# Attention terms of two graph layers: from row tiles on VectorE in the second, in four column groups of TensorE in the first

## The chip, the core and the metric

The kernel runs on one core of a Trainium2 chip. The core has TensorE (matrix products, into the accumulator memory PSUM), VectorE, ScalarE and GpSimd for elementwise work, and SyncE, which issues transfers. Each engine takes its own instructions in order and waits for the others by semaphores. In the profile they are PE (PEld is TensorE's loading of the stationary operand), DVE, ACT, POOL and SP. The metric is the time of one execution on the device in microseconds (us).

## What is computed

A graph network of two attention layers, followed by a transformer block (attention and a mixture of 8 experts), on 1250 nodes of 768 features, all in float32. The change is in the graph layers. Each does this, with 41,250 edges given as `src` and `dst`:

```python
def _gat_layer(x, W, a_src, a_dst, b, src, dst, n_nodes):
    h = x @ W
    e_src = h @ a_src
    e_dst = h @ a_dst
    e = jax.nn.leaky_relu(e_src[src] + e_dst[dst], NEG_SLOPE)
    m = jax.ops.segment_max(e, dst, num_segments=n_nodes)
    w = jnp.exp(e - m[dst])
    z = jax.ops.segment_sum(w, dst, num_segments=n_nodes)
    alpha = w / z[dst]
    out = jax.ops.segment_sum(h[src] * alpha[:, None], dst, num_segments=n_nodes)
    return out + b

h = _gat_layer(x, W1, att_src1, att_dst1, b1, src, dst, n_nodes)
h = jax.nn.relu(h)
out = _gat_layer(h, W2, att_src2, att_dst2, b2, src, dst, n_nodes)
```

The two attention terms of a node are `e_src` and `e_dst`. Since `h @ a = x @ (W @ a)`, the kernel never takes them from `h`: it computes the two vectors `W @ a_src` and `W @ a_dst` and multiplies the layer's input by them.

## The kernel before

Nodes are cut into NT = 10 tiles of T = 125, features into DC = 6 pieces of P = 128. Of a layer's input two forms occur: row tiles (125 nodes on partitions, 768 features along the row) and the transposed form `xT` (feature pieces on partitions, all 1250 nodes along the row). `CHUNKS` cuts the 1250 nodes into three pieces of 417, 417 and 416 columns.

**The vectors.** `attention_vectors` (L167) loads `a_src` and `a_dst` repeated on all partitions (`rep`) and has VectorE multiply every piece of `W` by them and sum (L183), twelve instructions a layer. The result, `wa`, has the features on partitions, two columns a piece.

**The terms.** `attention_terms` (L187) multiplies `xT` by these two columns, six matmuls a chunk that add up in PSUM (`pe`, L192), and ScalarE copies the two rows that come out into `er` (L195), which has 2 partitions and 1250 columns. It is a generator: each `next` issues one matmul. In the first layer two chunks are issued together (L361) ahead of the edge work (`win`, L364 to L380, and the transposes of `win`, L388), and the third is dealt out one matmul at a time among the counting of edges (L409 to L420: VectorE makes one-hot rows `ohp`, TensorE counts with 25 small matmuls `pc`). In the second layer all three chunks are issued together (L552) after the last tile of the first layer has been turned into `x1T`.

**A layer** (`gat_layer`, L472). Ten transposes turn `er` into `es`, nodes on partitions (`pec`, L479; copy L480). VectorE takes the largest source term per destination (`most`, L487 and L489, ten steps), from which come, by further turns and copies, the rows `rows` (L464 to L470). Then `rest()` projects the input, `h = x @ W` (`project`, `ph`, L203): seven tiles in the first layer, all ten in the second. Destination tiles are taken in three parts (4, 3 and 3 tiles). For each part ScalarE and VectorE make ten weight tiles `wt` (L517 to L522, 12 buffers), and for each destination tile TensorE adds up 20 matmuls (`pagg`, L529); VectorE divides (`rz`, L533) and adds the bias (`o`, L535). In the first layer `o` is transposed (`ptr`, L140) and ScalarE copies it through a ReLU into `x1T` (L297). With the first tile the second layer's weight `gw2` is loaded, over the first's, and its vectors are made (L549).

**What sets the order.** Tiles are written in program order, and a scheduler at build time fixes each engine's sequence by readiness and by that order. In the blocks under `manual_schedule` the order of the named engines is that of the code. The chip then runs each engine's sequence as it stands. A tile of a pool waits for its buffer: `gp` has two of each tag (`xr`, `row` for `o`, `e`), `gpt` has three PSUM buffers `tr` in the layers and two in the edge stage. Matmuls in float32 appear in the profile as two records each, transposes as one.

Of the kernel before, what the change touches and what calls it, by code (L numbers as in the profile page):

```python
# [10 lines left out]
F32 = mybir.dt.float32  # L11
# [6 lines left out]
ALU = mybir.AluOpType  # L18
AX = mybir.AxisListType
# [8 lines left out]
def gnn_ffn_kernel(  # L28
# [24 lines left out]
    nc = tc.nc  # L53
    N, D = x.shape
    E = src.shape[0]
    P = 128
    T = 125
    NT = N // T
    DC = D // P
# [42 lines left out]
    ident = const.tile([P, P], F32, name="ident")  # L102
# [57 lines left out]
    with tc.tile_pool(name="cnt", bufs=1) as cpool:  # L160

        cnt = cpool.tile([T, NT, N], U16, name="cnt")

        wa = cpool.tile([P, 2, DC, 2], F32, name="wa")
        er = cpool.tile([2, N], F32, name="er")

        def attention_vectors(layer, w, a_src, a_dst, pool, bufs):  # L167

            def load(a):
                rep = pool.tile([P, D], F32, tag="rep", name="rep", bufs=bufs)  # L170
                tc.keep_in_program_order((nc.sync if bufs > 1 else nc.scalar).dma_start(
                    rep, bass.AP(tensor=a.tensor, offset=a.offset, ap=[[0, P], [1, D]])))
                return rep

            reps = [load(a) for a in (a_src, a_dst)[:bufs]]
            if bufs > 1:
                yield None
            for i in range(2):
                if i == bufs:
                    reps.append(load(a_dst))  # L180
                for c in range(DC):
                    scr = pool.tile([P, D], F32, tag="scr", name="scr", bufs=1)
                    nc.vector.scalar_tensor_tensor(scr, w[:, c, :], 1.0, reps[i], op0=ALU.mult, op1=ALU.mult,  # L183
                                                   accum_out=wa[:, layer, c, i:i + 1])
                    yield None

        def attention_terms(layer, xT, psum):  # L187

            for c0, w in CHUNKS:
                pe = psum.tile([P, 4, P], F32, tag="tr", name="pe").rearrange("p a b -> p (a b)")  # L190
                for c in range(DC):
                    nc.tensor.matmul(pe[0:2, :w], wa[:, layer, c, :], xT[:, c, c0:c0 + w],  # L192
                                     start=(c == 0), stop=(c == DC - 1))
                    if c == DC - 1:
                        nc.scalar.copy(er[:, c0:c0 + w], pe[0:2, :w])  # L195
                    yield None

        def project(xT, w, h, psum, tiles):
# [16 lines left out]
        with tc.tile_pool(name="edge", bufs=1) as ep, \  # L215
# [53 lines left out]
            def find_rows():  # L269
                nc.vector.tensor_scalar(begun, nodes, head, None, ALU.is_gt)  # L270
                pk = epc.tile([P, 512], F32, tag="pc", name="pk")
                for t in range(NT):
                    nc.tensor.matmul(pk[:T, t:t + 1], begun[:, t * T:(t + 1) * T], oneb,
                                     start=True, stop=True)
                return pk

            def gather_row(t):
                krows[t] = op.tile([T, EC], F32, tag="kr", name="kr", bufs=LEAD)
                nc.gpsimd.indirect_dma_start(
                    out=krows[t], out_offset=None, in_=keys[0:E].rearrange("(p e) -> p e", p=T),  # L280
                    in_offset=bass.IndirectOffsetOnAxis(ap=row[:, t:t + 1], axis=0))
# [20 lines left out]
            xT = big.tile([P, DC, N], F32, tag="A", name="xnT")  # L302
# [4 lines left out]
            def spread(t):  # L307
                if t == len(xrows):
                    xn = op.tile([T, D], F32, tag="xn", name="xn", bufs=4)
                    split_rows(nc.sync if t % 2 == 0 else nc.scalar, xn, x[t * T:(t + 1) * T, :])  # L310
                    xrows.append(xn)
                stats[t] = ln_root(xrows[t])
# [14 lines left out]
            def vector(n):  # L327
                for _ in range(n):
                    next(vectors, None)

            fixed = {mybir.EngineType.PE, mybir.EngineType.DVE, mybir.EngineType.Pool}
            with tc.manual_schedule(engines=fixed):
                vector(1)
                pk = find_rows()
                spread(0)
                nc.vector.tensor_scalar(row, pk[:T, :NT], -1.0, None, ALU.add)
                nc.vector.tensor_scalar(edges, pk[:T, :NT], -1.0, float(EC), ALU.add, ALU.mult)
                for t in range(LEAD):
                    gather_row(t)
                nc.gpsimd.iota(upto, pattern=[[1, 2 * NT], [0, 5 * PG]], base=1, channel_multiplier=0,  # L340
                               allow_small_or_imprecise_dtypes=True)
                for t in range(4):
                    if t > 0:
                        spread(t)
                        normal(t - 1)
                normal(3)
                for t in range(4):
                    columns(t)
                for t in range(NT):
                    if 2 <= t <= 7:  # L350
                        spread(t + 2)
                    first_edges(t)
                    if t + LEAD < NT:
                        gather_row(t + LEAD)
                    if t % 3 == 0 and t // 3 < EARLY:
                        project(xT, gw, h, gpo, [t // 3])
                    vector(0 if t < 3 else 1 if t < 5 else 2)
                    if 2 <= t <= 7:
                        normal(t + 2)
                        columns(t + 2)  # L360
                terms = attention_terms(0, xT, gpt)  # L361
                for _ in range(2 * DC):
                    next(terms)
                nc.vector.tensor_tensor(win, win, node[:, :, None].to_broadcast([T, NT, SL]), ALU.subtract)  # L364
# [6 lines left out]
                                           accum_out=found)  # L371
# [12 lines left out]
            for u0 in range(0, NT // 2, 4):  # L384
                n = min(4, NT // 2 - u0)
                pt = gpt.tile([P, 4, P], F32, tag="tr", name="pl")
# [14 lines left out]
            with tc.manual_schedule(engines={mybir.EngineType.PE, mybir.EngineType.DVE}):  # L401
                for g in range(NP // PG):
# [12 lines left out]
                    for i in range(2):  # L415
                        c0 = (2 * u + i) * T + q0
# [34 lines left out]
        with tc.tile_pool(name="gwork", bufs=2) as gp, \  # L451
# [6 lines left out]
            def columns_to_rows(cols, o):  # L458

                for t0 in range(0, NT, 4):  # L460
# [8 lines left out]
                    else:  # L469
                        nc.scalar.copy(out_, pt[:T, :n, :T])  # L470

            def gat_layer(layer, rest, b):  # L472
                bias = gv.tile([T, D], F32, tag="bias", name=f"bias{layer}")
                nc.scalar.dma_start(bias, bass.AP(tensor=b.tensor, offset=b.offset, ap=[[0, T], [1, D]]))

                es = gv.tile([T, NT, 2], F32, tag="es", name=f"es{layer}")
                pt = gpt.tile([P, 4, P], F32, tag="tr", name="pec").rearrange("p a b -> p (a b)")
                for t in range(NT):
                    nc.tensor.transpose(pt[:T, 2 * t:2 * t + 2], er[:, t * T:(t + 1) * T], ident[0:2, 0:2])  # L479
                nc.scalar.copy(es.rearrange("p t i -> p (t i)"), pt[:T, :2 * NT])  # L480

                most = gv.tile([T, N], F32, tag="most", name=f"most{layer}")
                for t in range(NT):
# [4 lines left out]
                    else:  # L488
                        nc.vector.scalar_tensor_tensor(most, am[:, t, :], es[:, t, 0:1], most,  # L489
                                                       op0=ALU.add, op1=ALU.max)  # L490

                mx = gv.tile([T, NT], F32, tag="mx", name="mx")
                for t0 in range(0, NT, 4):
                    n = min(4, NT - t0)
                    pt = gpt.tile([P, 4, P], F32, tag="tr", name="pmx")
# [16 lines left out]
                for d0, nd in PARTS:  # L512
                    cs = slice(d0 * T, (d0 + nd) * T)
                    ws = []
                    for j in range(NT):
# [4 lines left out]
                                                       op0=ALU.min, op1=ALU.max)  # L520
                        wt = gp.tile([T, PW], F32, tag="wt", name="wt", bufs=12)
                        nc.vector.scalar_tensor_tensor(wt[:, :nd * T], e[:, 0, :nd * T], 1.0, cnt[:, j, cs],  # L522
                                                       op0=ALU.min, op1=ALU.mult)
                        ws.append(wt)
                    for d in range(d0, d0 + nd):
                        po = gpo.tile([T, 2, 512], F32, tag="po", name="pagg")
                        for s in range(2):
                            for j in range(NT):
                                nc.tensor.matmul(po[:, s, :DH + s], ws[j][:, (d - d0) * T:(d - d0 + 1) * T],  # L529
                                                 h[:, j, s * DH:(s + 1) * DH + s],  # L530
                                                 start=(j == 0), stop=(j == NT - 1))
                        rz = small.tile([T, 1], F32, tag="rz", name="rz")
                        nc.vector.reciprocal(rz, po[:, 1, DH:DH + 1])  # L533
                        o = gp.tile([T, D], F32, tag="row", name="o")
# [6 lines left out]
                project(xT, gw, h, gpo, range(EARLY, NT))  # L541
                return h

            x1T = None
            for t, o in gat_layer(1, rest_of_first, gb1):
                if t == 0:
                    x1T = big.tile([P, DC, N], F32, tag="A", name="x1T")
                    gw2 = load_big_weight(gW2, "gw2")
                    for _ in attention_vectors(1, gw2, ga_src2, ga_dst2, gp, 1):  # L549
                        pass  # L550
                transpose_rows(gpt, o, evict_to(x1T, t, AF.Relu))
            for _ in attention_terms(1, x1T, gpt):  # L552
                pass

            def all_of_second():
                h = node_rows("h2")
# [8 lines left out]
            pt = gpt.tile([P, 4, P], F32, tag="tr", name="pln")  # L565
# [3 lines left out]
            for t, o in gat_layer(2, all_of_second, gb2):  # L569
# [4 lines left out]
                xr = gp.tile([T, D], F32, tag="xr", name="xres")  # L574
# [208 lines left out]
    start = gate.tile([P, NE], F32, name="start")  # L783
# [27 lines left out]
    before = gate.tile([T, T], F32, name="before")  # L811
# [23 lines left out]
    with tc.tile_pool(name="proj", bufs=3, reuse_waits="tile") as pp, \  # L835
# [5 lines left out]
        w = load_expert(first_w, *expert(0))  # L841
# [81 lines left out]
        for t in range(NT):  # L923
            if t + 1 < NT:
# [8 lines left out]
                                       op0=ALU.add, op1=ALU.is_gt, accum_out=count)  # L933
# [10 lines left out]
    with tc.tile_pool(name="moe", bufs=2, reuse_waits="tile") as mp, \  # L944
# [66 lines left out]
        xr = fetch(xd[0:CAP, :], NS)  # L1011
# [21 lines left out]
        xT = turn(xr, NS)  # L1033
        for i, (e, n, _, _) in enumerate(jobs):
# [6 lines left out]
            if i + 1 < len(jobs):  # L1041
                _, m, ws, slots = jobs[i + 1]
                w = load_expert(mp.tile([P, 2 * DC * FF], F32, tag="w", name="we"), *ws)
                xr = fetch(slots(), m)
                xT = turn(xr, m)
# [33 lines left out]
```

## Time and profile before

| | us |
|---|---|
| median of 3 runs (lowest, highest) | 1541.48 (1539.98, 1541.97) |
| the profiled execution, on the device | 1540.1 |
| its span, first to last instruction | 1538.3 |

| engine | busy us | share of the span | instructions |
|---|---|---|---|
| PE | 1457.0 | 95% | 5981 |
| PEld | 782.8 | 51% | 5981 |
| DVE | 796.7 | 52% | 1285 |
| ACT | 597.8 | 39% | 950 |
| POOL | 433.9 | 28% | 287 |

Line groups that the change touches, in the profile's order: L192 `pe` in the first layer, 36 records, from 61.5 to 133.6 us; L192 in the second, 36 records, from 339.4 to 351.6; L479 `pec`, 10 records in each layer; L183 `scr`, 24 products of 0.957 us in both layers together, the second layer's from 208.6 to 224.0.

The graph layers take the first 581 us of the span. Shares are averages over stages with different limits: what an instruction costs is seen only where it stands in the chain of waits, that is, in the sequence of work followed back from the last instruction to whatever released each step. The granted TensorE clock over the whole span is 0.962 of full speed; it is at half in some stretches in which TensorE has little to do, the counting of edges among them.

### The profile page before, as it was taken

Reading aid. Unit: us, or ns where it says so; the run is one execution under the profiler, and the core shown is the slowest. Engines: PE = TensorE matmul, PEld = TensorE weight load, DVE = VectorE, ACT = ScalarE, POOL = GpSimd, SP = SyncE. Lnnn points to the kernel's source line nnn. Section 1 sums busy time; section 2 is a strip of 40 time slices with the busy share of each in tenths; the row PEclk is TensorE's granted clock in tenths of the full one; section 3 lists DMA queues with packets and bytes.
Section 4 is the critical chain, followed back from the end, with each engine's and each line's share of the span. In section 5 each row is a group of like instructions: output and inputs, shape, how many; then the busy total and the mean of one; then the engine's idle time right before and its main releaser. Section 6 shows DMA issues by size and latency. Waiting matters only on the chain.

```text
span 1538.3 us, 15938 instructions
## 1 busy us (share of the span) xinstructions
PE 1457.0 (95%) x5981; PEld 782.8 (51%) x5981; DVE 796.7 (52%) x1285; ACT 597.8 (39%) x950; POOL 433.9 (28%) x287
## 2 busy tenths in 40 slices
PE   5689999999999999999999999999988997799998
PEld 3376655555555555553444434334333665466565
DVE  4598633205326740117877877877888665011111
ACT  3222503202414621215655655655666354212121
POOL 6300000000000002004764664664666322122222
PEclk9856999999999999999999999999999997899999
DMA  7100010000021118940000000000030333745644
GB/s 215 32 1 31 11 72 0 0 11 2 1 81 56 56 44 338 408 175 23 1 21 1 21 0 21 1 21 1 0 101 1 126 118 120 292 166 179 222 150 142
DMA packets 48847, 125.49 MB, mean 82 GB/s; under 512 B 6103, under 2 KB 22680, under 8 KB 48768
## 3 DMA queue, kind: packets, MB, share of 16 engines
q1 hardware_dynamic: 30958, 55.99, 10.8%
q0 software_dynamic: 12688, 57.10, 9.8%
q10 hardware_dynamic: 5122, 11.36, 2.5%
q8 instruction: 48, 0.79, 0.2%
q14 instruction: 31, 0.25, 0.1%
HBM read 71.30 MB, written 57.60 MB: 84 GB/s over the span
## 4 chain that ended last, share of the span: by engine, by line
PE 70%; DVE 11%; issue 8%; DMA 5%; ACT 4%; POOL 1%; SPq 0%; POOLq 0%; DVEq 0%; ACTq 0%
PE pagg L529 12%; PE ph L203 8%; PE st L663 8%; PE pav L707 7%; PE pk L626 5%; PE pv L642 5%; PE phe L993 5%; PE poe L1002 5%; PE pq L626 4%; DVE sT L693 2%; DMA xd<-yn,slot 2%; PE pe L192 2%; PE pc L413 2%; PE po L851 2%; DMA xn<-in_x_dram 1%
## 5 line engine op out<-in xcount | busy, mean ns | idle before, releaser
L699 POOL TENSOR_TENSOR acc<-acc,sT 125x834 f32<-125x834 f32 (+1 forms) x139 | 273.2, 1965 | 10.9
L529 PE MATMUL pagg<-h,wt 125*125 125x385 f32 (+1 forms) x800 | 262.7, 486 | 0.4 <-DVE wt L522 0.4
L672 DVE TENSOR_TENSOR most<-most,st 125x834 f32<-125x834 f32 (+1 forms) x144 | 147.0, 1021 | 105.3 <-ACT sT L666 102.1
L529 PEld LDWEIGHTS pagg<-h,wt 125*125 125x125 f32 x800 | 147.4, 187 | 106.1 <-DVE wt L522 3.5
L693 DVE TENSOR_TENSOR sT<-sT,mb 125x834 f32<-125x834 f32 (+1 forms) x180 | 174.2, 1016 | 22.6 <-PE mb L688 22.6
L694 ACT ACTIVATE sT<-sT 125x834 f32<-125x834 f32 (+1 forms) x180 | 158.4, 900 | 49.0 <-DVE sT L693 48.6
L666 ACT COPY sT<-st 125x834 f32<-125x834 f32 (+1 forms) x180 | 151.7, 848 | 51.7 <-PE st L663 49.7
L663 PE MATMUL st<-qk 64*125 64x417 f32 (+1 forms) x720 | 163.7, 554 | 4.4 <-DVE most L672 4.3
L707 PE MATMUL pav<-sT,v 125*64 125x417 f32 (+1 forms) x720 | 151.5, 534 | 8.7 <-ACT sT L694 8.7
L604 POOL MEMSET zero<- 128x772 f32 x1 | 0.7, 742 | 520.6 <-PE ptr L140 520.6
L699 POOL TENSOR_TENSOR acc<-sT 125x834 f32<-125x834 f32 (+1 forms) x18 | 35.4, 1965 | 275.2 <-ACT sT L694 275.2
L663 PEld LDWEIGHTS st<-qk 64*125 64x125 f32 x720 | 56.3, 183 | 99.8 <-DVE most L672 43.4
L707 PEld LDWEIGHTS pav<-sT,v 125*64 125x64 f32 x720 | 42.7, 137 | 104.9 <-issue 43.7
L1002 PE MATMUL poe<-we,hT 128*128 128x384 f32 x264 | 88.8, 486 | 0.0
L626 PE MATMUL pq<-yT,wqk 128*128 128x417 f32 (+1 forms) x216 | 88.1, 534 | 0.0
L851 PE MATMUL po<-wp,aT 128*125 128x384 f32 x240 | 87.5, 498 | 0.0
L993 PE MATMUL phe<-xT,we 128*128 128x384 f32 (+1 forms) x288 | 86.6, 460 | 0.0
L1006 DVE SCALAR_TENSOR_TENSOR sofar<-poe,weight,sofar 128x768 f32<-128x768 f32 x25 | 25.4, 1018 | 116.8 <-PE poe L1002 109.8
L626 PE MATMUL pk<-yT,wqk 128*128 128x417 f32 (+1 forms) x216 | 84.0, 526 | 0.0
L203 PE MATMUL ph<-gw,xnT 128*125 128x384 f32 x240 | 82.5, 504 | 0.0
L642 PE MATMUL pv<-wv,yT 128*125 128x384 f32 x240 | 79.9, 490 | 1.4 <-issue 1.4
L203 PE MATMUL ph<-gw,x1T 128*125 128x384 f32 x240 | 78.6, 487 | 0.0
(219 smaller groups left out, 1737.1 us busy)
## 6 DMA issues: line engine op xcount, KB each, us to landing
xd<-zero POOLq DMA_DIRECT2D x8, 3860.0 KB
we<-in_L_ffn_W_dram SPq DMA_DIRECT2D x16, 1152.0 KB
xr<-xd SPq DMA_DIRECT2D x25, 386.0 KB
gw<-in_L_gnn_W_dram SPq DMA_DIRECT2D x2, 2304.0 KB
wqk<-in_L_ffn_Wqkv_dram SPq DMA_DIRECT2D x12, 384.0 KB
xres<-in_x_dram SPq DMA_DIRECT2D x10, 375.0 KB
xsd<-xres ACTq DMA_DIRECT2D x10, 375.0 KB
wv<-in_L_ffn_Wqkv_dram SPq DMA_DIRECT2D x1, 2304.0 KB
```

What stands on the lines that cost most here:

```text
L203: nc.tensor.matmul(po[:, s, :DH], xT[:, c, t * T:(t + 1) * T], w[:, c, s * DH:(s + 1) * DH], start=(c == 0), stop=(c == DC - 1))
L529: nc.tensor.matmul(po[:, s, :DH + s], ws[j][:, (d - d0) * T:(d - d0 + 1) * T], h[:, j, s * DH:(s + 1) * DH + s], start=(j == 0), stop=(j = ...
L626: nc.tensor.matmul(pq[:, :w], wqk[:, c, i, :], yT[:, c, c0:c0 + w], start=(c == 0), stop=(c == DC - 1))
L642: nc.tensor.matmul(pv[:T, s, :DH], yT[:, c, t * T:(t + 1) * T], wv[:, c, s * DH:(s + 1) * DH], start=(c == 0), stop=(c == DC - 1))
L663: nc.tensor.matmul(st[:T, i, :w], self.qk[r, 1, j * T:(j + 1) * T], self.qk[r, 0, self.c0:self.c0 + w], start=True, stop=True)
L666: nc.scalar.copy(s[:, :, :w], st[:T, :, :w])
L693: nc.vector.tensor_tensor(s[:, :, :w], s[:, :, :w], self.mb[:T, :, :w], ALU.subtract)
L694: nc.scalar.activation(s[:, :, :w], s[:, :, :w], AF.Exp)
L699: nc.gpsimd.tensor_tensor(self.acc[:, :, :w], prev[:, :, :w], s[:, :, :w], ALU.add)
L707: nc.tensor.matmul(self.pav[r, :w], v[:, j, hd0:hd0 + HD], s[:, i, :w], start=(j == 0), stop=(j == NT - 1))
L993: nc.tensor.matmul(ph[:, :n * P], w1[:, c, f * P:(f + 1) * P], xT[:, c, :n * P], start=(c == 0), stop=(c == DC - 1))
L1002: nc.tensor.matmul(po[:, d, :DH], hT[:, f, s * P:(s + 1) * P], w2[:, f, d * DH:(d + 1) * DH], start=(f == 0), stop=(f == FC - 1))
```

## The change

In the first layer the vectors lie in `wa1` with 32 columns a piece, of which 30 are zero, set once by GpSimd. The matmul of piece c now writes 32 PSUM partitions, beginning at 32 * (c % 4): four groups of partitions hold partial sums (pieces 0 and 4, 1 and 5, 2, 3). `er` has 128 partitions. The four partial sums are added when `er` is turned: in place of a transpose, a matmul with `four`, a 128 x 2 matrix of ones at the places of the two terms in each group, made from the identity.

In the second layer `attention_terms` and the turns of `er` are gone. The vectors `wa2` are turned after the first tile into rows repeated on 125 partitions, `wrow`: twelve transposes of a broadcast column (`pwr`), three copies by ScalarE. VectorE then takes both terms of a tile from its row tile `o`: ReLU, product and sum in one instruction for each term (`second_terms`), into `es2`, one tile behind the transposes. Its scratch, and the loads and scratch of `attention_vectors` in this layer, use the buffers of tag `xr`.

```diff
--- before.py
+++ after.py
@@ -161,13 +161,18 @@
 
         cnt = cpool.tile([T, NT, N], U16, name="cnt")
 
-        wa = cpool.tile([P, 2, DC, 2], F32, name="wa")
-        er = cpool.tile([2, N], F32, name="er")
-
-        def attention_vectors(layer, w, a_src, a_dst, pool, bufs):
+
+        wa1 = cpool.tile([P, DC, 32], F32, name="wa1")
+        nc.gpsimd.memset(wa1, 0.0)
+        wa2 = cpool.tile([P, 2, DC], F32, name="wa2")
+        er = cpool.tile([P, N], F32, name="er")
+
+        es2 = cpool.tile([T, NT, 2], F32, name="es2")
+
+        def attention_vectors(layer, w, a_src, a_dst, pool, bufs, tags=("rep", "scr")):
 
             def load(a):
-                rep = pool.tile([P, D], F32, tag="rep", name="rep", bufs=bufs)
+                rep = pool.tile([P, D], F32, tag=tags[0], name="rep", bufs=bufs if layer == 0 else None)
                 tc.keep_in_program_order((nc.sync if bufs > 1 else nc.scalar).dma_start(
                     rep, bass.AP(tensor=a.tensor, offset=a.offset, ap=[[0, P], [1, D]])))
                 return rep
@@ -179,20 +184,21 @@
                 if i == bufs:
                     reps.append(load(a_dst))
                 for c in range(DC):
-                    scr = pool.tile([P, D], F32, tag="scr", name="scr", bufs=1)
+                    scr = pool.tile([P, D], F32, tag=tags[1], name="scr", bufs=1 if layer == 0 else None)
                     nc.vector.scalar_tensor_tensor(scr, w[:, c, :], 1.0, reps[i], op0=ALU.mult, op1=ALU.mult,
-                                                   accum_out=wa[:, layer, c, i:i + 1])
+                                                   accum_out=wa1[:, c, i:i + 1] if layer == 0 else wa2[:, i, c:c + 1])
                     yield None
 
-        def attention_terms(layer, xT, psum):
+        def attention_terms(xT, psum):
 
             for c0, w in CHUNKS:
                 pe = psum.tile([P, 4, P], F32, tag="tr", name="pe").rearrange("p a b -> p (a b)")
                 for c in range(DC):
-                    nc.tensor.matmul(pe[0:2, :w], wa[:, layer, c, :], xT[:, c, c0:c0 + w],
-                                     start=(c == 0), stop=(c == DC - 1))
+                    g = c % 4
+                    nc.tensor.matmul(pe[32 * g:32 * g + 32, :w], wa1[:, c, :], xT[:, c, c0:c0 + w],
+                                     start=(c < 4), stop=(c + 4 >= DC))
                     if c == DC - 1:
-                        nc.scalar.copy(er[:, c0:c0 + w], pe[0:2, :w])
+                        nc.scalar.copy(er[:, c0:c0 + w], pe[:, :w])
                     yield None
 
         def project(xT, w, h, psum, tiles):
@@ -358,7 +364,7 @@
                     if 2 <= t <= 7:
                         normal(t + 2)
                         columns(t + 2)
-                terms = attention_terms(0, xT, gpt)
+                terms = attention_terms(xT, gpt)
                 for _ in range(2 * DC):
                     next(terms)
                 nc.vector.tensor_tensor(win, win, node[:, :, None].to_broadcast([T, NT, SL]), ALU.subtract)
@@ -469,15 +475,22 @@
                     else:
                         nc.scalar.copy(out_, pt[:T, :n, :T])
 
+
+            four = gv.tile([P, 2], F32, name="four")
+            nc.vector.tensor_reduce(four, ident.rearrange("p (g k) -> p k g", g=4)[:, 0:2, :], AX.X, ALU.add)
+
             def gat_layer(layer, rest, b):
                 bias = gv.tile([T, D], F32, tag="bias", name=f"bias{layer}")
                 nc.scalar.dma_start(bias, bass.AP(tensor=b.tensor, offset=b.offset, ap=[[0, T], [1, D]]))
-
-                es = gv.tile([T, NT, 2], F32, tag="es", name=f"es{layer}")
-                pt = gpt.tile([P, 4, P], F32, tag="tr", name="pec").rearrange("p a b -> p (a b)")
-                for t in range(NT):
-                    nc.tensor.transpose(pt[:T, 2 * t:2 * t + 2], er[:, t * T:(t + 1) * T], ident[0:2, 0:2])
-                nc.scalar.copy(es.rearrange("p t i -> p (t i)"), pt[:T, :2 * NT])
+                es = es2
+                if layer == 1:
+
+                    es = gv.tile([T, NT, 2], F32, name="es1")
+                    pt = gpt.tile([P, 4, P], F32, tag="tr", name="pec").rearrange("p a b -> p (a b)")
+                    for t in range(NT):
+                        nc.tensor.matmul(pt[:T, 2 * t:2 * t + 2], er[:, t * T:(t + 1) * T], four,
+                                         start=True, stop=True)
+                    nc.scalar.copy(es.rearrange("p t i -> p (t i)"), pt[:T, :2 * NT])
 
                 most = gv.tile([T, N], F32, tag="most", name=f"most{layer}")
                 for t in range(NT):
@@ -541,16 +554,34 @@
                 project(xT, gw, h, gpo, range(EARLY, NT))
                 return h
 
-            x1T = None
+            def second_terms(t, o):
+
+                for i in range(2):
+                    scr = gp.tile([T, D], F32, tag="xr", name="scr")
+                    nc.vector.scalar_tensor_tensor(scr, o, 0.0, wrow[:, i * D:(i + 1) * D], op0=ALU.max, op1=ALU.mult,
+                                                   accum_out=es2[:, t, i:i + 1])
+
+            x1T = before = None
             for t, o in gat_layer(1, rest_of_first, gb1):
                 if t == 0:
                     x1T = big.tile([P, DC, N], F32, tag="A", name="x1T")
                     gw2 = load_big_weight(gW2, "gw2")
-                    for _ in attention_vectors(1, gw2, ga_src2, ga_dst2, gp, 1):
+                    for _ in attention_vectors(1, gw2, ga_src2, ga_dst2, gp, 1, ("xr", "xr")):
                         pass
                 transpose_rows(gpt, o, evict_to(x1T, t, AF.Relu))
-            for _ in attention_terms(1, x1T, gpt):
-                pass
+                if t == 0:
+
+                    wrow = gv.tile([T, 2 * D], F32, name="wrow")
+                    flat = wa2.rearrange("p i c -> p (i c)")
+                    for k0 in range(0, 2 * DC, 4):
+                        pt = gpt.tile([P, 4, P], F32, tag="tr", name="pwr")
+                        for k in range(4):
+                            nc.tensor.transpose(pt[:T, k, :], flat[:, k0 + k:k0 + k + 1].to_broadcast([P, T]), ident)
+                        nc.scalar.copy(wrow[:, k0 * P:(k0 + 4) * P], pt[:T].rearrange("p a b -> p (a b)"))
+                else:
+                    second_terms(*before)
+                before = t, o
+            second_terms(*before)
 
             def all_of_second():
                 h = node_rows("h2")
```

## The prediction

> **What bounds it now.** I read the page's chain of waits first, then that chain for the first 470 us in order of time, then busy time by stage. The page's chain by engine:
>
> ```profile
> PE 70%; DVE 11%; issue 8%; DMA 5%; ACT 4%; POOL 1%; SPq 0%; POOLq 0%; DVEq 0%; ACTq 0%
> ```
>
> and the pieces of the chain around the change (start us, length us, engine, tile, line, records):
>
> ```profile
> 61.54 10.26 PE pe L192 x24
> 71.80 0.33 PE psum L376 x2
> ...
> 105.02 1.47 PE pe L192 x2
> ...
> 138.43 2.25 PE pec L479 x10
> 140.69 21.27 PE ph L203 x60
> ...
> 338.79 0.64 PE ptr L140 x6
> 339.43 12.69 PE pe L192 x36
> 352.11 4.71 PE ph L203 x14
> 356.82 0.17 PE pln L566
> 356.99 1.09 PE pec L479 x10
> ...
> 379.45 53.54 PE ph L203 x166
> 432.99 21.31 PE pagg L529 x66
> ```
>
> The reader is to see that both attention terms (L192) and both turns of `er` (L479) lie on the chain themselves, and that after the second terms TensorE goes on with `ph` until 433, with `pagg` right behind it. Busy time by stage (length, then PE, PEld, DVE, ACT, POOL with counts, granted clock, DMA share, GB/s) says the same:
>
> ```profile
> 72.40:136.50 64.10, 54.42 (x642) 44.51 (x642) 55.86 (x36) 16.95 (x52) 0.00 (x0) 0.53 0.01 2
> 136.50:200.00 63.50, 61.56 (x208) 37.87 (x209) 39.72 (x66) 25.15 (x42) 0.00 (x0) 0.94 0.07 25
> 200.00:339.00 139.00, 137.87 (x466) 81.34 (x465) 40.77 (x79) 25.72 (x51) 0.00 (x0) 1.00 0.06 20
> 339.00:433.00 94.00, 93.79 (x316) 51.57 (x315) 34.31 (x46) 28.05 (x48) 0.00 (x0) 1.00 0.02 5
> ```
>
> From 200 to 433 TensorE is full at clock 1.00 and VectorE is idle two thirds of the time. Work taken off TensorE here is time; work put on VectorE is not, as long as TensorE doesn't wait for it.
>
> **Second layer's terms leave TensorE: -13.8.** The 36 records of `pe` (12.69) and the 10 of `pec` (1.09) go: 13.78 us. What is late next? `es2` is whole two VectorE products after the last `o` (337.09 + 1.02): a product of this kind is L183, 0.957 and an accumulator read, 1.00 from start to start, so at 340.2, against 358.3 now. Today `wt` of all ten tiles of the first part is done at 396.0, 37.6 after `es`; then 378. `ph` would end at 433.0 - 13.8 = 419.2: 41 us of cover. Nothing becomes late; the shift goes through whole, because `pagg` waits for the end of `ph` both times.
>
> **The 20 products of `second_terms`: 0.** Two per tile, 2.0 us. VectorE waits 12.34 us for `pagg` in front of most `rz`, so they fit. At a change of part (248 to 262) VectorE refills `wt`; there the product for tile 3 may fall among them, but `wt` 8 and 9 are made at 256.2 and 257.3 and `pagg`, at 0.65 a tile from about 254.7, reaches them near 261. Were the cover gone, a tile would cost its 2.0. Each `o` now lives until the next tile's turn; two buffers do for that. Their scratch takes the two `xr` buffers, so the loads of `xres` that SP issued at 137.2 go out near 340; they are needed after 455.
>
> **Twelve turns `pwr`: +1.3.** Six `ptr` took 0.64, so 12 take 1.28, on a full TensorE. Three ScalarE copies of 128x512 (L470's of 125x500 are under 0.6) lie in ScalarE's idle. A wait is added: TensorE waits for `wa2`, and `pagg` of tile 1 stands behind it. VectorE now finishes the second half of those vectors at 223.96. If all 12 stand right behind `ptr` of tile 0 (which ends at 217.15), TensorE stands 6.8 us. Ends: +1.3 and +8.1. I take the lower: `ptr` of later tiles is put four records into the next tile's `pagg` and waits at most 0.57, tile 0's is put ten records in and waits for nothing, so the order given to TensorE follows VectorE's times well here.
>
> **First two chunks in column groups: -5.6.** Now 24 records one after another. With four groups, c = 0..3 run together and c = 4, 5 together: 2 rounds x 2 passes x 2 chunks = 8 slots. The weight loads show the record spacing: 0.35 for two, then 0.69 to 65.03 and 0.65 to 65.68 (the clock was at half there), then 0.35. Eight slots end at 66.03; `psum` starts at about 66.2, not at 71.80: 5.6 us. Behind it stands VectorE's `win` (L374), done at 65.66, so no more than 6.1 can come of it; `found` is there at 64.3.
>
> Is it so, side by side? No row has four groups. The nearest has two:
>
> ```profile
> 698.99 0.20 PEld L707 LDWEIGHTS pav<-sT,v 125*64 125x64 f32 x4 [0.60 <-ACT sT L694]
> 698.99 1.62 PE L707 MATMUL pav<-sT,v 125*64 125x417 f32 x8
> ```
>
> Eight records of the same 417 columns, 64 output partitions each, in 1.62: less the last one's 0.51, 1.11 us from the first start to the last, three spacings of 0.37 and not seven of 0.35 (2.45). So pairs start together, fp32 and all. [...] But all four loads above fall in 0.20 us while the first pair (0.51) runs: the row decides, 5.6. If only two groups ever run together, it is 12 slots: 67.4, a gain of 4.2. Ends: -2.9 (pairs and loads, with a margin) and -6.1.
>
> **Third chunk: +0.8.** Its six matmuls go one at a time into the count (`next(terms)` at g % 4 == 3), so nothing runs beside them; four are in the chain at 1.47. [...] The row between `st` (64 rows) and `pq` (128) shows 0.1 a change: 0.8, which I take. Ends 0 and 1.6.
>
> **`es1` by matmul: +1.1.** A transpose is one record, an fp32 matmul two (psum L376 is x2). Ten turns at half clock took 2.25; twenty records, each with a load of 125 columns, take about 4.4: +2.2. The clock hands some back: 60 `ph` in 21.27, against 0.3225 each later (96 in 30.96), means about six at 0.64. If the clock rises as long after the count as now, `pec` uses 2.2 us of that slow time, and 3.4 `ph` run at full clock instead: -1.1. Net +1.1; ends 0 and +3.4 (no refund, and TensorE waiting 1.2 for `four`, if that stands behind the ten L448 adds, done at 139.4). VectorE's `most` moves with it; `wt` has 12 us of cover before `ph` ends at 200.4.
>
> **At nothing:** the memset of `wa1` (POOL is idle from 7.8 to 14.5), the copies of `er` on 128 partitions in place of 2, `attention_vectors` on `xr` buffers (the second row still loads when the first six products are done).
>
> **Sum:** -13.8 - 5.6 + 1.3 + 0.8 + 1.1 = -16.2. The profiled execution took 1540.1 (span 1538.3 and 1.8 around it), so 1523.9; it stood 1.4 below the median of 1541.5, so against the median **1525.3**.
>
> **Rivals.**
> *The groups don't run side by side.* For it: no four-group row, fp32 in two passes. Against: `pav`. The 5.6 stays: 1530.9. Chance 0.13.
> *`pwr` holds TensorE up* by the 6.8 above, one early place in a queue that can't be passed: 1532.1. Chance 0.13.
> *Slower: VectorE's new filler stands ahead of `o`.* `second_terms` and the second layer's `most` (nine of its ten steps need only finished tiles, 1.53 each) may be put between `rz` and `o`. `ptr` is only four records (1.3 us) behind, so each us is TensorE's: 3.5 a tile over nine tiles, 31.8, gives 1557.1. It decides from 1.8 a tile. For it: the filler has no other engine. Against: in the trace `o` follows `rz` directly, even amid the `wt` refill. Chance 0.04.
> My forecast 0.68; 0.02 for what I don't see.
>
> **Range and chances.** Best ends: -13.8 - 6.1 + 1.3 + 0 + 0, and up to 1.9 of slow clock gone: -20.5, 1521. Worst of the small terms without a rival: -13.8 - 2.9 + 1.3 + 1.6 + 3.4 = -10.4, 1531. With both mild rivals in it, one after the other: 1520 to 1534. A measurement tells some 0.2% (3.1 us) from no change. Faster 0.93 (forecast and mild rivals), same 0.03, slower 0.04.
>
> **What would show it.** `pe` with x36 gone from the second layer, and `ph` following `ptr` of tile 9 without a break; `pe` x24 at 61.5 in some 4.5 us, its records starting in fours and twos; `pec` in layer one with 20 records; 12 `pwr` with no idle before them; `ptr` of tiles 1 to 9 waiting no longer than now. I am wrong if `pwr` shows several us of TensorE idle, if `pe` keeps its 0.35 spacing, or if `rz` and `o` come apart.

## The result, and the profile after

The changed kernel takes 1530.1 us (median of 4 runs, 1527.9 to 1531.9), the one before 1541.6; the ratio is 0.9927, 95% interval 0.9909 to 0.9944. A second set (e0 below) gives 0.9923, 0.9911 to 0.9936. So it is 11.5 to 12.6 us faster, where 16.2 were forecast: the direction and the range held, the size was about 4 us too large. The profiled execution of the changed kernel took 1527.9 with a span of 1526.1, 12.2 below the profiled execution of before.

The page's chain by engine:

```profile
PE 71%; DVE 9%; issue 8%; DMA 6%; ACT 4%; POOL 1%; POOLq 0%; SPq 0%; ACTq 0%; DVEq 0%
```

and the chain of waits in order of time, at the places shown of before (start us, length us, what):

```profile
62.32 3.01 PE pe L198 x24
...
81.09 1.52 PE pe L198 x2
...
132.68 5.48 PE ph L209 x8
138.16 2.16 PE pec L491 x20
...
211.75 0.64 PE ptr L140 x6
212.40 0.74 PE pwr L579 x6
213.13 1.29 PE pagg L542 x4
214.57 0.65 PE pagg L542 x2
215.21 0.35 PE pwr L579
...
337.75 5.78 DMA lnr<-in_L_ffn_ln_b_dram
343.66 0.21 PE pln L597
343.87 1.28 PE pmx L510 x10
...
350.28 68.37 PE ph L209 x212
418.65 21.31 PE pagg L542 x66
```

The 24 records of the first two chunks take 3.0 us in place of 10.3. The second layer's 36 records are gone, but in their place stands something that was not in the chain before: a transfer. TensorE's own timeline in that stretch shows it (start, length, line, output and input, records; in brackets the idle time before, and what ended it):

```profile
335.86 0.81 PE L140 MATMUL ptr<-ident,o 125*128 125x125 f32 x6
336.50 4.68 PE L209 MATMUL ph<-gw,x1T 128*125 128x384 f32 x14
343.66 0.21 PE L597 MATMUL pln<-ident,lnr 24*128 24x24 f32 x1 [2.48 <-DMA lnr<-in_L_ffn_ln_b_dram]
```

`pln` turns the layer-norm parameters, which are first used at 440.3, 96 us later. TensorE waits 2.48 us for them because `pln` stands there in its sequence, with most of `ph` behind it.

Putting equal milestones of the two profiled executions beside each other (start times from the trace, differences worked out; `pl` are the transposes of `win`, `po` is the projection behind attention) gives the account:

| step | before, us | after, us | change | forecast |
|---|---|---|---|---|
| start of the first `pe` | 61.5 | 62.3 | +0.8 | 0 |
| first `pe` to first `pl` | 10.8 | 4.0 | -6.8 | -5.6 |
| first to last `pc` (the count, with the third chunk) | 56.5 | 56.7 | +0.3 | +0.8 |
| last `pc` to first `pagg` (with `pec`) | 64.1 | 65.1 | +1.0 | +1.1 |
| `ptr` of tile 0 to tile 1 (with `pwr`) | 12.3 | 14.3 | +2.0 | +1.3 |
| `ptr` of tile 9 to the second layer's `pagg` | 94.2 | 82.6 | -11.6 | -13.8 |
| that `pagg` to `po` (to the end of attention) | 746.3 | 748.0 | +1.7 | 0 |
| `po` to the end | 359.2 | 359.6 | +0.3 | 0 |

Stretches left out differ by less than 0.1. The sum is -12.3. The first row is no effect of the change that could be told from chance: over all twelve profiles of this document the first `pe` starts between 59.7 and 62.3. Two rows carry the shortfall: the second layer gave 2.2 less, and 1.7 went missing in a stage that the change doesn't touch.

### The profile page after: what moved, and what is told of

Its sections match the earlier page's. It is cut to its first block, busy times and chain, and to the rows that moved or that the text cites. A ratio compares the mean times of both kernels' runs of the same rounds, so it can differ in the third digit from the quotient of the medians.

```text
span 1526.1 us, 15935 instructions
## 1 busy us (share of the span) xinstructions
PE 1442.0 (94%) x5957; PEld 781.8 (51%) x5957; DVE 813.5 (53%) x1326; ACT 598.0 (39%) x949; POOL 433.7 (28%) x288
## 4 chain that ended last, share of the span: by engine, by line
PE 71%; DVE 9%; issue 8%; DMA 6%; ACT 4%; POOL 1%; POOLq 0%; SPq 0%; ACTq 0%; DVEq 0%
PE pagg L542 12%; PE ph L209 9%; PE st L694 8%; PE pav L738 7%; PE pk L657 5%; PE pv L673 5%; PE phe L1024 5%; PE poe L1033 5%; PE pq L657 4%; PE pc L419 2%; DMA xd<-yn,slot 2%; DVE sT L724 2%; PE po L882 2%; ACT sT L697 1%; DVE most L703 1%
## 5 line engine op out<-in xcount | busy, mean ns | idle before, releaser
L546 DVE RECIPROCAL rz<-pagg 125x1 f32<-125x1 f32 x20 | 3.3, 166 | 141.5 <-PE pagg L542 141.5
```

## The experiments

All but e0 are edits of the changed kernel; their diffs are excerpts.

**e0, the changed kernel again.** 

> The changed kernel once more. If the time lost after the graph layers (1.5 us near the end of attention, where one more stretch at half clock was recorded than before) is the chance [...], another execution shows the same graph part (the second layer's aggregation starting at 418.7 +-1) and a different number of half-clock stretches there, and the median lies 11 to 13 us below that of before. If the change itself causes it, the same loss of 1.4 to 2.1 us is there again at the same place.

1528.3 (5 runs). Nearly the same `pagg` start, 418.5, but by another road. The row from `ptr` of tile 9 to `pagg` took 84.2, not 82.6, and the terms 4.49, not 3.0. Busy time by stretch behind `pln` in this execution (length, PE, PEld, DVE, ACT, POOL with counts, granted clock, DMA share, GB/s) tells the first:

```profile
342.06:343.20 1.14, 1.14 (x10) 1.11 (x11) 0.27 (x1) 0.18 (x1) 0.00 (x0) 1.00 0.38 137
343.20:346.60 3.40, 3.40 (x9) 1.97 (x8) 1.91 (x7) 0.28 (x1) 0.00 (x0) 0.51 0.24 89
346.60:350.00 3.40, 3.34 (x23) 2.65 (x22) 0.68 (x1) 2.78 (x6) 0.00 (x0) 0.99 0.00 0
```

TensorE is busy throughout all three stretches, but in the second, a microsecond after it has stood still, it was granted 0.51 of its clock. So the wait at `pln` can cost more than itself: 2.4 us and then some 1.5. The loss in attention is there again, 748.1, with the same 6.83 us at half clock near 1118 where the profile of before records 3.41. This speaks against pure chance, but see below.

**e1, the first layer's part alone.** The second layer keeps the old terms:

```diff
-                nc.vector.scalar_tensor_tensor(scr, o, 0.0, wrow[:, i * D:(i + 1) * D], op0=ALU.max, op1=ALU.mult,
-                                               accum_out=es2[:, t, i:i + 1])
+                nc.tensor.matmul(pe[0:2, :w], wa2[:, c, :], xT[:, c, c0:c0 + w],
+                                 start=(c == 0), stop=(c == DC - 1))
```

> Only the first layer's part: 32-column groups and the turn by matmul; the second layer keeps its 36 records of terms and its transposes. By the trace of the changed kernel this part is worth 4.8 us (the first aggregation starts at 195.6 in place of 200.4): 1536.9. If the prediction's terms were right instead, 3.7 (5.6 - 0.8 - 1.1): 1538. If the gain of the first layer were only luck with the clock, under 2 us: above 1539.6.

1534.8, ratio 0.9960 (0.9947 to 0.9973): 6.1 us below before (1540.9), with an interval of 4.2 to 8.2. That takes in the 4.8 that the trace gave the part and lies above the 3.7 of the forecast's terms. From `ptr` of tile 9 to `pagg` it takes 94.2 like before, `pln` does not wait, and attention takes 746.1.

**e2, the second layer's part alone.** The first layer has its two columns and transposes again:

```diff
-                    nc.tensor.matmul(pe[32 * g:32 * g + 32, :w], wa1[:, c, :], xT[:, c, c0:c0 + w],
+                    nc.tensor.matmul(pe[0:2, :w], wa1[:, c, :], xT[:, c, c0:c0 + w],
```

> Only the second layer's part: two-column terms and transposes in the first layer as before. By the trace of the changed kernel: -11.6 in the second layer, +2.0 for the twelve turns, so 9.6 us: 1532.0. If the second layer's shortfall belonged to the first layer's part, the full 13.8 - 1.3 = 12.5 would appear: 1529.1. e1 and e2 add up to the whole change if the parts don't touch each other: 4.8 + 9.6 = 14.4 in the graph part.

1533.5, ratio 0.9959 (0.9946 to 0.9971): 7.4 us with an interval of 4.5 to 8.3, so less than 9.6 and far from 12.5. Its trace has the wait at `pln` followed by half clock: 84.1 from `ptr` of tile 9 to `pagg`, a gain of 10.1, less 2.2 for `pwr`. The parts add up within the noise: 6.05 + 7.37 = 13.4 against 12.6 for the whole on the same chip. The shortfall belongs to the second layer's part.

**e3, the layer-norm loads before the first layer.**

```diff
+            lnr = gv.tile([4 * DC, P], F32, name="lnr")
+            for i, a in enumerate((ln1_g, ln1_b, ln2_g, ln2_b)):
...
             x1T = before = None
             for t, o in gat_layer(1, rest_of_first, gb1):
...
-            lnr = gv.tile([4 * DC, P], F32, name="lnr")
-            for i, a in enumerate((ln1_g, ln1_b, ln2_g, ln2_b)):
...
```

> As the changed kernel, but the five loads of the layer-norm parameters and the router (lnr, wr) are issued before the first layer instead of after it. Theory: TensorE stands 2.5 us at pln (L597) because its data lands late, and everything behind it in TensorE's queue waits. Then those 2.5 us go: the aggregation of the second layer starts 2.5 us earlier relative to the last ptr, and the median is 2 to 2.6 us below the changed kernel's. Rival: the wait is cover for something else that is late (most, VectorE), and another wait takes its place: less than 0.5 us gained.

1525.2, ratio to before 0.9902 (0.9888 to 0.9917): 3.1 us below e0 on the same chip, a little more than expected, though the two intervals overlap. TensorE's timeline:

```profile
336.86 0.24 PE L598 MATMUL pln<-ident,lnr 24*128 24x24 f32 x1
337.03 2.20 PE L209 MATMUL ph<-gw,x1T 128*125 128x384 f32 x6
```

No wait, and none took its place: 80.2 from `ptr` of tile 9 to `pagg`, 14.0 less than before the change. That is the 13.8 of the forecast. Against e0's profile the row is 4.0 shorter, more than the 2.4 of the wait: the half clock behind it is gone as well.

**e4, xres behind lnr.** Is it the lost cover, or did something delay the transfer?

```diff
-                nc.sync.dma_start(xr, x[t * T:(t + 1) * T, :])
+                (nc.scalar if t < 2 else nc.sync).dma_start(xr, x[t * T:(t + 1) * T, :])
```

> As the changed kernel, but the two loads of xres that now go out at 336.4, because their buffers serve the second layer's products until then, are issued by ScalarE behind the loads of lnr instead of by SyncE just ahead of them. Theory: lnr (issued 336.7 to 338.1) lands late, at 343.5, since it shares the DMA engines with 750 KB of xres; before it landed 4.6 us after the first issue, now 6.9. Then lnr lands near 341.3 and TensorE's idle time at pln falls from 2.5 to 0.5 us or less. Rival: the landing takes as long as it takes and only the cover (12.7 us of terms on TensorE) is gone: the wait stays between 2 and 2.6 us.

One run, 1525.0. The timeline of issues and of `pln` (ACTq is ScalarE's queue of transfers):

```profile
337.05 0.29 ACTq L593 DMA_DIRECT2D lnr<-in_L_ffn_ln_g_dram  x1
...
338.92 0.76 ACTq L606 DMA_DIRECT2D xres<-in_x_dram  x2
...
341.45 0.24 PE L597 MATMUL pln<-ident,lnr 24*128 24x24 f32 x1
```

`lnr` is issued no earlier than in the changed kernel and `pln` keeps its place behind 14 records of `ph`, but there is no wait: the data is there 4.4 us after the first issue at the latest, where the changed kernel needed 7.0. The row is 80.2 again. So 12 KB of parameters were late because two transfers of 375 KB went out just ahead of them. A third one of that size, the bias rows, stands ahead of `lnr` on ScalarE's queue in the changed kernel and in e4; with it alone in front, in e4, there is no wait. e4 moves `xres` to a later time and to ScalarE's queue at once, so which of the two helped is not told. In the changed kernel the loads of `xres` are issued at 336.4:

```profile
336.37 1.14 SPq L606 DMA_DIRECT2D xres<-in_x_dram  x2
...
336.70 0.29 ACTq L593 DMA_DIRECT2D lnr<-in_L_ffn_ln_g_dram  x1
```

Before the change they had left at 137.2; they moved because the `xr` buffers now serve the second layer's products until the last tile. Lost cover it was not. In the kernel before, `lnr` was issued behind the copy of the last terms, and TensorE came to `pln` 4.6 us later, behind the same 14 records of `ph` (the 4.6 of the expectation is this distance, not the landing). In the changed kernel it came to `pln` 4.5 us after the first issue:

```profile
137.21 0.65 SPq L575 DMA_DIRECT2D xres<-in_x_dram  x2
...
352.15 0.29 ACTq L562 DMA_DIRECT2D lnr<-in_L_ffn_ln_g_dram  x1
...
356.75 0.24 PE L566 MATMUL pln<-ident,lnr 24*128 24x24 f32 x1
```

**e5, the twelve turns behind tile 1.**

```diff
-                if t == 0:
+                if t == 1:
                     wrow = gv.tile([T, 2 * D], F32, name="wrow")
...
-                else:
+                if t >= 1:
                     second_terms(*before)
```

> As the changed kernel, but the twelve turns pwr stand together behind the transposes of tile 1, when all of wa2 is long there. Theory: of the 2.0 us that they cost, 1.3 are the turns themselves, 0.7 the waits for VectorE at each of the six single ones: the stretch from ptr of tile 0 to ptr of tile 2 is 0.7 us shorter than in the changed kernel. Rival: each break of a run of matmuls costs as much by itself: no change in that stretch, or less than 0.3 us.

One run, 1528.9. First the changed kernel's `pwr` by line query, idle time in front of its weight loads and what ended it; then e5's timeline:

```profile
  DVE scr L188: 1.3, 3
  ACT wrow L580: 0.7, 1
```

```profile
224.97 1.55 PE L579 MATMUL pwr<-ident,wa 128*125 128x128 f32 x12
226.36 13.08 PE L542 MATMUL pagg<-h,wt 125*125 125x384 f32 x40
```

From `ptr` of tile 0 to tile 2 it is 27.2 in place of 27.8: 0.6 saved. Together the turns cost 1.4, scattered among the products of VectorE 2.0 (2.3 in e0). Over all ten tiles 0.4 of the saving is left, as e5 loses 0.2 at a later change of part.

**e6 and e7, fewer groups.** Two groups:

```diff
-                    g = c % 4
+                    g = c % 2
...
-                                     start=(c < 4), stop=(c + 4 >= DC))
+                                     start=(c < 2), stop=(c + 2 >= DC))
```

> As the changed kernel, but two column groups (c % 2) in place of four. If all groups run side by side, a chunk takes 3 rounds of two passes instead of 2: 24 records of pe in 12 slots, 4.3 us at full clock and up to 1.8 us more at half clock; four groups took 3.0 at full clock. If only two ever run together, two groups and four take the same time: 3.0.

One group, `g = 0`, with `start=(c == 0), stop=(c == DC - 1)`:

> As the changed kernel, but all pieces in one column group of 32 (weights of 32 columns, one result in 32 partitions): nothing runs side by side. 24 slots: 8.5 us at full clock, up to 10.3 with half-clock stretches as before the change; start to start 0.35. If the gain came from the width of the weights or of the copy, it would be 3 to 4.

One run each, 1532.7 and 1536.1. The first two chunks in TensorE's timeline, of e0, e6 and e7:

```profile
60.29 4.49 PE L198 MATMUL pe<-xnT,wa 128*32 128x417 f32 x24 [0.29 <-issue]
```

```profile
61.31 5.90 PE L198 MATMUL pe<-xnT,wa 128*32 128x417 f32 x24 [0.29 <-issue]
```

```profile
60.69 10.26 PE L198 MATMUL pe<-xnT,wa 128*32 128x417 f32 x24 [0.29 <-issue]
```

Each of the three has most or all of a 3.41 us stretch at half clock in it; the profile of the changed kernel happened to have none (3.00). One group takes what two columns took before the change, 10.26 to the hundredth: the width of the weights costs nothing, and all of the gain is in running side by side. Two groups lie where 12 slots lie, four where 8 do. In the changed kernel the first eight weight loads come within 0.19 us, and eight records of 0.51 take 0.91 in all, two rounds of four:

```profile
62.29 0.19 PEld L198 LDWEIGHTS pe<-xnT,wa 128*32 128x32 f32 x8 [0.49 <-issue]
62.32 0.91 PE L198 MATMUL pe<-xnT,wa 128*32 128x417 f32 x8 [0.29 <-issue]
```

**e8, the third chunk in front.**

```diff
-                for _ in range(2 * DC):
+                for _ in range(3 * DC):
                     next(terms)
```

> As the changed kernel, but the third chunk of the first layer's terms follows the first two at once, in four groups, and not one matmul at a time among the counting. Theory: there it costs six times 1.53 us of TensorE with nothing beside it; in front it is four slots, 1.4 us (2.8 at half clock). The count is then bound by VectorE's one-hot rows (25 x 1.9 and 5 x 1.47, 54.9 us), so from the first to the last pc it takes 53 to 54 in place of 56.7; net 1 to 2 us gained. Rival: the six matmuls lie in gaps in which TensorE waits for VectorE anyway: the count stays within 1 us of 56.7 and the 1.4 in front are lost.

1526.2, ratio to before 0.9903 (0.9886 to 0.9919); e0's was 0.9923. By the ratios that is 3 us more, by the medians (13.7 and 12.6 below before) 1, and the intervals overlap: the times alone don't show a gain. The trace is clearer. The 36 records in front take 6.08, 1.6 more than e0's 24, and the count from first to last `pc` takes 52.7 in place of 56.7. Busy time over the count of the changed kernel and of e8:

```profile
70.00:130.40 60.40, 53.79 (x637) 44.43 (x637) 53.71 (x32) 16.03 (x49) 0.00 (x0) 0.50 0.01 1
```

```profile
70.00:128.20 58.20, 45.49 (x625) 43.66 (x625) 55.21 (x35) 15.54 (x48) 0.00 (x0) 0.51 0.01 2
```

In the first, TensorE and VectorE are both busy 54 of 60 us and get in each other's way (at half clock the count is no stretch in which TensorE has little to do); in the second VectorE alone is the bound, at 95%. The six single matmuls were not free filler.

**e9, e3, e5 and e8 together.** 

> The changed kernel with three edits at once: the layer-norm loads before the first layer, the twelve turns behind tile 1, the third chunk in front. If the pieces add up: 2.4 and the 1.5 of slow clock that follows the wait at pln, 0.6, and 1 to 2, so 4 to 6.5 us below the changed kernel's 1528.3 to 1530.1: 1522 to 1525.

1521.2 (1520.1 to 1522.8), ratio to before 0.9875 (0.9859 to 0.9892), 18.7 us below before and just past the fast end of what was expected: the best version here, faster than both kernels. `pwr` stands together for 1.39, `pln` does not wait, and `pagg` of the second layer starts at 412.1.

## Why the prediction was right, and where its size was off

*The direction and the main term held.* TensorE was the bound from 136 to 433 us (by the forecast's table busy 293 of 296.5 us), and what left it there came out of the time; in the count before that, VectorE bounds as much (e8). With the wait at `pln` removed (e3, e4) the second layer gives 14.0 against the 13.8 of the forecast.

*The step that failed* is the one on the transfers: "so the loads of `xres` that SP issued at 137.2 go out near 340; they are needed after 455", counted under a heading of 0. The time was right (336.4) and so was the need. The question asked was whether `xres` would come too late; the one not asked was whom it would make late. The four small loads of `lnr` leave from 336.7 on, and one TensorE instruction waits for them in front of 70 us of work. The forecast's "Nothing becomes late" looked only at VectorE's chain to `wt`. The price: 2.4 us of wait, shown by e3 and e4, and 1.5 more in those executions in which half clock follows it (five of the seven traces with the wait: e0, e2, e5, e6, e7; not the first profile and not e8). It would account for most of the 2.2 us by which the first profile stands below its own median; that was not shown.

Where the wait falls sorts these seven traces. In a trace's clock records the half-clock stretches begin whole multiples of one length apart: in e0 at 42.88, 59.94, 70.18 and 343.25, so 17.06, 10.24 and 273.07 us apart, which are 5, 3 and 80 times 3.413. Continue this grid over the wait: in the five, at least 2.2 us of it lie between two grid lines. In the first profile a line at 343.00 cuts the wait (341.18 to 343.66) into 1.8 and 0.7, in e8 it is cut into 1.5 and 0.9. No run moved the grid, so this is a regularity of seven traces and not a tested cause.

*The first two chunks*: right. Against the 10.8 of before the row is 6.8 shorter in the first profile and 5.3 in e0, where 5.6 were forecast; the difference is whether a half-clock stretch falls on it. Eight slots were taken, with a half-clock stretch, as 4.5 us; e0 shows 4.49, and the profile without the stretch 3.0. The row of pairs (`pav`) was the right witness, and weight loads did not come between matmuls: eight of them fall within 0.19 us, and the eight records that they serve take 0.91. That loads might take up TensorE's time, which set the forecast's smaller end of 2.9, was the author's estimate. The first rival falls with e7: without groups side by side the terms take 10.26.

*The third chunk*: +0.3 against 0.8. The forecast put 0.1 us on each of eight changes between matmuls of different shape; that the 0.1 measured between `st` and `pq` (in the profile of before 0.45 us from start to start at 697.4, then 0.35) holds between the widths of 32 and 128 columns was the author's estimate, as was the end of 1.6, 0.2 a change. No loss of either size shows. What the forecast took as given, that this chunk is dealt out singly, was the larger thing: e8 takes some 2.5 us net from it by the trace (4.0 less in the count, 1.6 more in front).

*`es1` by matmul*: +1.0 against 1.1. Twenty records took 2.16; the schedule put eight `ph` ahead of them (`four` is made at 133.6, the first `ph` starts at 132.7; that this is the scheduler's reason was not tested), so the half clock fell on `ph` and not on `pec`. The net was right, the course was not. Over the ten traces with this matmul the stretch takes 63.8 to 66.9, so this is no better than luck within 1.5 us.

*`pwr`*: 2.0 against 1.3. The second rival was right in kind, not in size: the weight loads of the turns stood idle 1.3 us at three turns for VectorE's vectors and 0.7 at a fourth for a PSUM buffer. Most of that lay behind running matmuls: against the turns in one block (1.4, e5) TensorE lost 0.6, as the turns were spread among `pagg`.

*VectorE's products*: 0, as forecast. Twenty of 0.955 us fit, and `ptr` of tiles 1 to 9 comes at the same distances as before. `o` follows `rz` as it did; the forecast's "directly, even amid the `wt` refill" was misread, since at a change of part an `e` of 0.5 us stands between them in the kernel before (`rz` at 254.64, `o` at 255.31) as in this one. The slower rival didn't come, though the scheduler did move steps of the second layer's `most` into the first layer, behind the products.

*Outside the sum*: 1.7 us in attention, where the forecast had nothing. It comes with one more half-clock stretch there, in the two profiles of the changed kernel and in e8. The other eight variants (e1 to e7 and e9), most of which have the same graph layers but for one edit, take 746.1 to 746.7 like before. So it does not look like an effect of the change as such. The position of the 3.41 us grid sorts these too: counted from the second layer's `pagg`, half clock begins 699.1 to 699.5 us later in the three, 697.8 to 698.9 in before and seven others, 700.2 in e1. That this position is the cause was not tested.

## What to carry to other kernels

When a buffer is given a second use, follow the transfer that used to fill it: ask when it now leaves and what leaves beside it, not only when it is needed. A small transfer that an in-order engine waits for should be loaded long before its place in the sequence: here 12 KB behind larger loads cost TensorE 2.4 us and more. And once a matmul has been made cheap by running it beside others, take back the places where it was dealt out singly as filler.

## What the runs showed of the hardware

Four column groups of 32 in float32 run fully side by side: 24 records in 8 slots (3.0 us at full clock), 12 slots for two groups and 24 for one (5.90 and 10.26 us with a half-clock stretch in each), and eight weight loads, two to each of the four groups, come within 0.19 us.

In five of seven traces with an idle time of some 2.4 us on TensorE, a stretch of 3.4 us at half clock began 0.2 to 1.2 us after the work's resuming (in e0 2.36 us of idle time, work again from 342.06, half clock from 343.25): those in which at least 2.2 us of the idle time lay within one piece of a 3.41 us grid. Whether it came changed between executions of the same program: in the first profile 2.48 us of idle time were followed by full clock (1.00 from 343.6 to 347). The stretches at half clock recorded here, 3.41, 6.83 and 27.31 us among them, last 1, 2 and 8 times 3.413 us.
